# Moving two matrix operands 64 bytes further: g at 128 bytes behind y, the turned adjacency at 384 bytes in its room

## The chip, the cores and the metric

The kernel runs on one core of one Trainium2 chip. Four of the core's engines matter here: TensorE (PE in the profile, with its weight loads as PEld), VectorE (DVE), ScalarE (ACT) and the DMA queues. The metric is the device time of one execution in microseconds; each figure is the median of several runs. Within the kernel, addresses count bytes inside one of the 128 partitions of the on-chip memory SBUF; a tile has the same address in every partition.

## What is computed

Sixty-four graphs of 256 nodes with 512 features each pass two layers. All of it is float32.

```
h   = relu(layernorm(x))                       # x: (64, 256, 512)
q, k, v = h Wq^T, h Wk^T, h Wv^T               # 512 x 512 weights
rel = adj^T * (q k^T)                          # 256 x 256 per graph
rel = rel / norm(rel, over the last axis)
x   = x + rel v
h   = relu(layernorm(x))
x   = x + (adj h) W + bias                     # W: 512 x 512
```

## The kernel before

Two graphs are taken at a time, so there are 32 passes (`pairs`, `i` from 0 to 31). With M = Wq^T Wk formed once, a pass does these stages on TensorE, every product written through `mm` (line 255) as "stationary operand times moving operand":

- `g_stage` (line 405): g = M h, turned. Moving operand: h, 512 columns. 48 products.
- `v_stage` (line 416): v. Moving operand: Wv, 512 columns; stationary: h. 48 products.
- `scores` (line 429): the scores q k^T as g times h. Stationary: 128 columns of g; moving: 256 columns of h. 48 products in a pass, 1536 in all.
- `attend` (line 500): normalised scores times v, 512 columns moving.
- `gather` (line 544): y = adj h of the second layer. Stationary: 128 columns of the rows kept in `late` (four of which live in `v_low`); moving: 256 columns of the turned adjacency `adjt`. 32 products in a pass, 1024 in all.
- `mix` (line 571): y times W. Stationary: y; moving: W, 512 columns. 48 products.

Most float32 operands are held as parts named u, l and s (`split_right_ps`, `split_left_ps`), so that three products on parts make one product of nearly full precision. Each product has its own weight load, and the load of the next product's stationary operand runs while the present product streams its moving operand.

The order of instructions on every engine is fixed when the program is built: `Plan.order` simulates the engines with a cost for each operation (0.231 us for a 512-column product, `HALF` = 0.1185 us for a 256-column one) and sorts the operations by the start times it finds. Costs and dependences are named by hand; addresses don't enter.

What matters for the change is where the operands lie. g and y share one room of 2048 + `BEHIND` elements for each part (tags `gy_u`, `gy_l`, `gy_s`): `as_y` takes the first 2048 elements, `as_g` the 2048 that begin `BEHIND` elements later. With `BEHIND` = 16, g begins 64 bytes behind y. The room of the turned adjacency has 512 + 128 elements, and the adjacency begins at element P - 16 = 112 of it, byte 448.

The pool lays the rooms one behind the other in the order in which they are first asked for, each rounded up to 32 bytes. Between the start of `gy_u` and that of `gy_l` lie 8256 bytes of `gy_u`, 384 bytes of layer-norm statistics (two times 96 + 32 + 32 + 32) and 64 bytes of `norms`: 8704 = 17 times 512. Between `gy_l` and `gy_s` lie 8256 + 384 + 64 (`ones` and `low_max`), again 8704. The unused room `level` of 104 elements (416 bytes) brings the rooms behind it back to the same residue. So all large rooms, m, wv, w, h, hs, rel, v_low, late, gy and adjt, begin at one and the same place modulo 512 bytes; call it 0. In that count, modulo 512:

| product | stationary operand | moving operand | distance (stationary minus moving) |
|---|---|---|---|
| all with 512 columns | 0 | 0 | 0 |
| scores | 64 (g) | 0 (h) | 64 |
| gather | 0 (late, v_low) | 448 (adjacency), that is -64 | 64 |

`ident` (for 60 transposes on TensorE), `wq_last`, `wk_last`, `bias_bc` and `low_any` lie between `gy_s` and `level`, 96 bytes off this grid.

Of the kernel before, what the change touches and what calls it, by code (L numbers as in the profile page):

```python
# [113 lines left out]
def kernel(  # L114
# [12 lines left out]
    P = 128  # L127
    B, N, D = x.shape
    DC = D // P
    NC = N // P  # L130
    NB = 2
# [11 lines left out]
    def room(name, *shape, dtype=F32, tag=None):  # L143
        return pool.tile([P, *shape], dtype, name=name, tag=tag or name)

    def parts_room(name, *shape, tag=None):
        return [room(f"{name}_{k}", *shape, dtype=F32R, tag=f"{tag or name}_{k}") for k in "uls"]
# [16 lines left out]

    BEHIND = 16
    w_p = parts_room("w", DC, D)

    def as_y(tile):  # L170
        return tile[:, : DC * T].rearrange("p (d t) -> p d t", d=DC)

    def as_g(tile):
        return tile[:, BEHIND : BEHIND + DC * T].rearrange("p (d t) -> p d t", d=DC)

    def norm_rooms(j):
        return [(room(f"st{j}{n}", TC, 6), room(f"mv{j}{n}", TC, 2), room(f"rs{j}{n}", TC), room(f"nb{j}{n}", TC))
                for n in range(2)]
    wq_room = room("wq_sb", DC * T + BEHIND, tag="gy_u")
    stats = [norm_rooms(0)]  # L180
    norms = [room(f"rn{n}", NB, NC) for n in range(2)]
    wk_room = room("wk_sb", DC * T + BEHIND, tag="gy_l")
    stats.append(norm_rooms(1))
    ones, low_max = room("ones", 1), room("low_max", 1)
    gy_s = room("gy_s", DC * T + BEHIND, dtype=F32R)
    wq_sb, wk_sb = as_y(wq_room), as_y(wk_room)
    low_any = pool.tile([1, 1], I32, name="low_any")
    bias_bc = room("bias_bc", D)
    ident = room("ident", P)
    wq_last, wk_last = room("wq_last", D), room("wk_last", D)  # L190
    room("level", 104)

    rooms = {}

# [25 lines left out]
    def by_pe(i):  # L220

        return i < 2 or i + 1 == NP
# [58 lines left out]
    def load(plan, i, src=None, name="fresh"):  # L281

        dst = fresh if name == "fresh" else ring[i % 2]
        plan.add("SP", 0.65, lambda: SP.dma_start(out=dst, in_=xs[i]), [], keys(name, TC), lands=5.5)
# [24 lines left out]
    def h_rows(plan, i, src=fresh, name="fresh"):  # L309
        relu, needs = norm(plan, i, 0, src, name)  # L310
        for c in range(TC):
            plan.add("ACT", 0.72, lambda c=c: relu(h_rel[:, c, :] if name == "x0" else h_cols[:, c], c),
                     [(name, c), *needs, *([("h_rel", 0)] if c else [])], [("h_rel", c)] if c else keys("h_rel", TC))

    def h_place(plan, early=8.0):
        place(plan, flat_rel, flat_blocks, keys("h_rel", TC), "blocks", 2.3, early)
# [28 lines left out]
    def finish(plan):  # L345
        while waiting:
            waiting.pop(0)()
# [274 lines left out]
    def before_pairs():  # L622
        A.activation(norms[1][:, 0, 0:1], ones, AF.Sqrt)
        for _ in range(8):
            mm(bank[7][:, :P], warm, warm, True)
        V.tensor_single_scalar(low, adj_low[:, 0].bitcast(I32), 0xFFF, op=ALU.bitwise_and)
        V.tensor_reduce(low_max, low, axis=mybir.AxisListType.X, op=ALU.max)
        m_products(0)
        mm(bank[7][0:1, 0:1], low_max, ones, True)
        V.tensor_copy(low_any, bank[7][0:1, 0:1])  # L630
        for m in range(NC):
            for n in range(NC):
                nc.tensor.transpose(bank[6][:, ts(m * NC + n, P)], adj_sb[:, n, ts(m, P)], ident)
        for e in range(1, DC - 1):
            m_products(e)
        plan = Plan()
        h_rows(plan, 0, ring[0], "x0")
        plan.run()

    with tc.manual_schedule(engines=in_order):  # L640
        before_pairs()
    gy = [*(room(f"gy_{k}", DC * T + BEHIND, dtype=F32R) for k in "ul"), gy_s]
    g_p, y_p = [as_g(part) for part in gy], [as_y(part) for part in gy]
    rel_p = [room(f"rel_{k}", NB, NC, NC, P, dtype=F32R) for k in "ul"]
    adjt = []
# [4 lines left out]
    def first_turn(plan):  # L650

        u, l = h
        for d in range(DC):
            ps, key = next_bank(turned=True)

            def go(ps=ps, d=d):
                for c in range(TC):
                    nc.tensor.transpose(ps[:, ts(c, P)], h_rel[:, c, ts(d, P)], ident)
            plan.add("PE", 0.44, go, keys("h_rel", TC), [key])
            plan.add("ACT", 0.49, lambda ps=ps, d=d: A.activation(  # L660
                u[:, d], ps, AF.Copy, scale=NEAR), [key], [("h_u", d)])
            plan.add("DVE", 0.63, lambda ps=ps, d=d: V.tensor_sub(
                l[:, d], ps, f(u[:, d])), [key, ("h_u", d)], [("h_l", d)])
        for k in range(2):
            kept = [(f"h_{q}", d) for q in "ul" for d in (2 * k, 2 * k + 1)]
            plan.add("DVE", 1.14, lambda k=k: h_third(k), kept, [("h_s", 2 * k), ("h_s", 2 * k + 1)])

    def last_m(plan):
        for i in range(DC):
            plan.add("PE", 0.86, lambda i=i: m_products(DC - 1, (i,)), [], [("bank", i)])  # L670
            split_right_ps(plan, bank[i], ("bank", i), [lambda at, q=q: q[:, at, :] for q in m_p],
                           [[("m_u", i)], [("m_l", i)], [("m_s", i)]], i)
# [16 lines left out]
    def turn_wv(plan):  # L689
        for d in range(DC):  # L690
            ps, key = next_bank(turned=True)

            def go(ps=ps, d=d):
                for e in range(DC):
                    nc.tensor.transpose(ps[:, ts(e, P)], wv_sb[:, e, ts(d, P)], ident)
            plan.add("PE", 0.44, go, placed_all, [key])
            split_right_ps(plan, ps, key, [lambda at, q=q: q[:, at, :] for q in wv_p],
                           [[("wv_u", d)], [("wv_l", d)], [("wv_s", d)]], d)

    def split_w(plan):  # L700
        for d in range(DC):
            split_right_ps(plan, w_sb[:, d], [("x1", d)], [lambda at, q=q: q[:, at, :] for q in w_p],
                           [[("w_u", d)], [("w_l", d)], [("w_s", d)]], d)

    def pairs(exact):
        count["bank"] = 4
        waiting.clear()
        rooms.clear()
        plan = Plan()
        turned_adj = room("adjt_r", NC * N + P, dtype=F32R, tag="adjt") if exact else room("adjt", NC * N + P)  # L710
        adjt[:] = [turned_adj[:, P - 16 : P - 16 + NC * N].rearrange("p (c n) -> p c n", c=NC)]
        plan.add("ACT", 0.49, lambda: A.copy(adjt[0].rearrange("p m n -> p (m n)"), bank[6]), [("bank", 6)], ["adjt"])
        first_turn(plan)
        last_m(plan)
        count["bank"] = 4
        turn_wv(plan)
        h_rows(plan, 1)
        h_place(plan, 25.0)
        load(plan, 2)
        first_g(plan)  # L720
        v_stage(plan, 0, exact, (0, 1))
        scores(plan, 0)
        v_stage(plan, 0, exact, (2, 3))
        turn_scores(plan, 0)
        finish(plan)
        h_turn(plan)
        h_parts(plan)
        split_w(plan)
        plan.add("ACT", 0.58, lambda: A.activation(bias_bc, bias_bc, AF.Copy, scale=1.0 / ONE), [], ["bias"])
        attend(plan, 0, exact)  # L730
        for i in range(1, NP):
            last = i + 1 == NP
            load(plan, i, name=f"x{i % 2}")
            if not last:
                h_rows(plan, i + 1)
                h_place(plan)
            if i + 2 < NP:
                load(plan, i + 2)
            g_stage(plan, i)
            v_stage(plan, i, exact, (0,))  # L740
            v_stage(plan, i, exact, (1,), hold=True)
            scores(plan, i)
            gather(plan, i - 1, exact)
            while held:
                held.pop(0)()
            if by_pe(i):
                turn_scores(plan, i)
            v_stage(plan, i, exact, (2, 3))
            if not last:
                if not by_pe(i):  # L750
                    turn_scores(plan, i)
                waiting.append(lambda: (h_turn(plan), h_parts(plan)))
                mix(plan, i - 1)
            attend(plan, i, exact)
            if last:
                mix(plan, i - 1)
                gather(plan, i, exact)
            store(plan, i - 1)
        mix(plan, NP - 1)
        finish(plan)  # L760
        with tc.manual_schedule(engines=in_order):
            plan.run()
# [33 lines left out]
```

## Time and profile before

| what | value |
|---|---|
| median of 3 runs | 1561.38 us (1560.41 to 1562.69) |
| the profiled execution | 1560.76 us |
| its span, first to last instruction | 1559.0 us |
| mean granted TensorE clock | 0.999 |
| scores: matmul rows with 256 columns | 3 x 512, mean 281 ns |
| gather: matmul rows with 256 columns | 896 of late (mean 277 ns), 128 of v_low (mean 283 ns) |
| matmul rows with 512 columns | mean 389 to 391 ns |

Matmuls overlap, so a row's mean duration of one instruction isn't what a product costs. What it costs is the time from its start to the start of the next one. In a timeline, whose rows merge consecutive equal instructions, that is the difference between the starts of two rows divided by the count of the first.

### The profile page before, as it was taken

The numbers are of one execution on the slowest core, as the hardware profiler recorded it, in microseconds if no ns is written. First come the engines' busy times: TensorE is split into PE (matmuls) and PEld (weight loads), VectorE is DVE, ScalarE is ACT, GpSimd is POOL, SyncE is SP. The second block draws the span as 40 slices with busy tenths as digits, with TensorE's granted clock in tenths as the row PEclk, the third lists the DMA queues.
The fourth block names the chain that finished last, engine by engine and source line by source line (L and its number), as shares of the span: only waits on it lengthen the run. The fifth ranks groups of instructions, "written<-read, shape, count | busy, mean of one in ns | idle before, by whom it ended". The sixth has DMA issues, their size and how long they took to land.

```text
span 1559.0 us, 22543 instructions
## 1 busy us (share of the span) xinstructions
PE 1548.2 (99%) x8046; PEld 1323.5 (85%) x8046; DVE 1355.3 (87%) x2419; ACT 1022.7 (66%) x1941; POOL 24.3 (2%) x39
## 2 busy tenths in 40 slices
PE   9999999999999999999999999999999999999998
PEld 6788888888888888888888888888888888888886
DVE  6997889898889988898988899888989888989786
ACT  5567666666667676666676675766666766666654
POOL 0000000000000000000000000000000000000000
PEclk9999999999999999999999999999999999999999
DMA  5321333223333223333233332233332233322211
GB/s 199 112 83 41 122 111 120 77 71 110 118 113 119 66 78 117 114 117 90 72 96 118 112 122 68 77 114 114 116 106 71 81 121 111 120 71 76 85 55 56
DMA packets 91112, 153.63 MB, mean 99 GB/s; under 512 B 17136, under 2 KB 32240, under 8 KB 90992
## 3 DMA queue, kind: packets, MB, share of 16 engines
q1 hardware_dynamic: 80768, 116.46, 24.7%
q0 software_dynamic: 8432, 32.51, 5.7%
q10 hardware_dynamic: 1792, 3.15, 0.6%
q8 instruction: 65, 1.06, 0.3%
q14 instruction: 55, 0.45, 0.1%
HBM read 70.78 MB, written 33.55 MB: 67 GB/s over the span
## 4 chain that ended last, share of the span: by engine, by line
PE 95%; DVE 3%; DMA 1%; ACT 0%; issue 0%; ACTq 0%; DVEq 0%
PE bank L255 95%; DMA bias_bc<-in_L_gnn_bias_dram 1%; DMA x_ring<-in_x_dram 1%; DVE late_parts L266 0%; DVE late_parts L268 0%; DVE rel_s_parts L470 0%; DVE st L292 0%; DVE rel_l L475 0%; DVE gy_l L275 0%; DVE m_l L268 0%; DVE gy_l L268 0%; DVE wv_l L268 0%; DVE ht L322 0%; DVE wv_s L266 0%; DVE m_s L266 0%
## 5 line engine op out<-in xcount | busy, mean ns | idle before, releaser
L361 ACT ACTIVATE bank<-bank 128x512 f32<-128x512 f32 x572 | 333.5, 583 | 307.8 <-PE bank L255 304.2
L255 PE MATMUL bank<-wv_s,hs 128*128 128x512 f32 x512 | 137.8, 391 | 0.0
L255 PE MATMUL bank<-wv_u,h_u 128*128 128x512 f32 x512 | 137.5, 390 | 0.0
L255 PE MATMUL bank<-wv_l,h_l 128*128 128x512 f32 x512 | 136.9, 389 | 0.0
L255 PE MATMUL bank<-w_u,gy_u 128*128 128x512 f32 x512 | 136.9, 389 | 0.0
L255 PE MATMUL bank<-w_l,gy_l 128*128 128x512 f32 x512 | 136.9, 389 | 0.0
L255 PE MATMUL bank<-h_l,m_l 128*128 128x512 f32 x512 | 136.6, 389 | 0.1
L255 PE MATMUL bank<-w_s,gy_s 128*128 128x512 f32 x512 | 136.7, 389 | 0.0
L255 PE MATMUL bank<-h_u,m_u 128*128 128x512 f32 x512 | 136.5, 389 | 0.0
L255 PE MATMUL bank<-hs,m_s 128*128 128x512 f32 x512 | 136.4, 389 | 0.0
L266 DVE SCALAR_TENSOR_TENSOR gy_s<-gy_u,bank 128x512 fp32r<-128x512 f32 x128 | 86.2, 675 | 43.0 <-ACT gy_u L265 43.0
L255 PEld LDWEIGHTS bank<-h_l,m_l 128*128 128x128 f32 x512 | 96.0, 188 | 20.4 <-DVE h_l L339 0.5
L255 PEld LDWEIGHTS bank<-wv_l,h_l 128*128 128x128 f32 x512 | 96.1, 188 | 20.2
L255 PEld LDWEIGHTS bank<-h_u,m_u 128*128 128x128 f32 x512 | 96.0, 188 | 20.2 <-ACT m_u L265 0.2
L255 PEld LDWEIGHTS bank<-w_l,gy_l 128*128 128x128 f32 x512 | 96.1, 188 | 20.0
L255 PEld LDWEIGHTS bank<-hs,m_s 128*128 128x128 f32 x512 | 96.1, 188 | 19.9
L255 PEld LDWEIGHTS bank<-w_u,gy_u 128*128 128x128 f32 x512 | 96.0, 188 | 20.0
L255 PEld LDWEIGHTS bank<-w_s,gy_s 128*128 128x128 f32 x512 | 96.0, 188 | 20.0 <-ACT bank L361 0.2
L255 PE MATMUL bank<-adjt_r,late_parts 128*128 128x256 f32 x896 | 112.6, 277 | 0.0
L255 PEld LDWEIGHTS bank<-wv_s,hs 128*128 128x128 f32 x512 | 93.8, 188 | 18.3 <-ACT bank L361 0.7
L255 PEld LDWEIGHTS bank<-wv_u,h_u 128*128 128x128 f32 x512 | 93.7, 188 | 17.7
L255 PEld LDWEIGHTS bank<-adjt_r,late_parts 128*128 128x128 f32 x896 | 107.3, 188 | 0.0
(110 smaller groups left out, 3072.3 us busy)
## 6 DMA issues: line engine op xcount, KB each, us to landing
fresh<-in_x_dram SPq DMA_DIRECT2D x31, 1024.0 KB, 5.7
blocks<-h_rel SPq DMA_DIRECT2D x496, 64.0 KB, 2.0
x_ring<-in_x_dram SPq DMA_DIRECT2D x31, 1024.0 KB, 8.0
out_dram<-x_ring POOLq DMA_DIRECT2D x31, 1024.0 KB, 5.4
h_rel<-h_rel SPq DMA_DIRECT2D x464, 32.0 KB, 1.8
blocks<-in_L_gnn_Wv_dram ACTq DMA_DIRECT2D x1, 1024.0 KB, 11.1
x_ring<-in_L_gnn_weight_dram SPq DMA_DIRECT2D x1, 1024.0 KB, 12.3
out_dram<-x_ring SPq DMA_DIRECT2D x4, 256.0 KB, 2.3
```

The lines of the kernel that those rows point to most:

```text
L255: nc.tensor.matmul(out, left, right, start=first, stop=True, skip_group_check=True)
L266: plan.add("DVE", 0.63, lambda: V.scalar_tensor_tensor(s(), f(u()), ONE, ps, op0=ALU.mult, op1=ALU.subtract), [*key, *ku], ks)
L361: plan.add("ACT", 0.49, lambda: A.activation(ps, ps, AF.Copy, scale=ONE), [], [key])
```

## The change

`BEHIND` becomes 32, so g begins 128 bytes behind y, and the rooms of `gy` grow by 64 bytes each. The adjacency begins at element P - 32 = 96 of its room, byte 384. `norms`, `ones` and `low_max` move behind `gy_s`, which leaves 8320 + 384 = 8704 bytes between the starts of the gy rooms, and `level` shrinks by 192 bytes, which is what the three gy rooms have grown. All rooms ahead of `gy_u` and behind `level`, and the three gy rooms themselves, keep their addresses; `bias_bc`, `ident`, `wq_last`, `wk_last` and `low_any` move by 192 bytes. No operation is added, removed or put in another order.

```diff
-    BEHIND = 16
+    BEHIND = 32
...
     stats = [norm_rooms(0)]
-    norms = [room(f"rn{n}", NB, NC) for n in range(2)]
     wk_room = room("wk_sb", DC * T + BEHIND, tag="gy_l")
     stats.append(norm_rooms(1))
-    ones, low_max = room("ones", 1), room("low_max", 1)
     gy_s = room("gy_s", DC * T + BEHIND, dtype=F32R)
     wq_sb, wk_sb = as_y(wq_room), as_y(wk_room)
+    norms = [room(f"rn{n}", NB, NC) for n in range(2)]
+    ones, low_max = room("ones", 1), room("low_max", 1)
...
-    room("level", 104)
+    room("level", 56)
...
-        adjt[:] = [turned_adj[:, P - 16 : P - 16 + NC * N].rearrange("p (c n) -> p c n", c=NC)]
+        adjt[:] = [turned_adj[:, P - 32 : P - 32 + NC * N].rearrange("p (c n) -> p c n", c=NC)]
```

In the count of the table above, after the change:

| product | stationary operand | moving operand | distance |
|---|---|---|---|
| all with 512 columns | 0 | 0 | 0 |
| scores | 128 (g) | 0 (h) | 128 |
| gather | 0 (late, v_low) | 384 (adjacency), that is -128 | 128 |

## The prediction

> **What bounds the kernel now.** First the busy times and the chain of work that ended last:
>
> ```profile
> PE 1548.2 (99%) x8046; PEld 1323.5 (85%) x8046; DVE 1355.3 (87%) x2419; ACT 1022.7 (66%) x1941; POOL 24.3 (2%) x39
> ...
> PE 95%; DVE 3%; DMA 1%; ACT 0%; issue 0%; ACTq 0%; DVEq 0%
> ```
>
> TensorE never rests and is 95% of the chain. The waits of TensorE confirm it: the longest in total is 1.2 us, once, on the DVE. So what counts is the sum of the start-to-start times of 8046 products, and a nanosecond on each 256-column product (1536 in scores, 1024 in gather) is 2.56 us.
>
> Next the timeline of TensorE through the 256-column part of an ordinary pass (start, duration, what, count):
>
> ```profile
> 600.38 1.07 PE L255 MATMUL bank<-wv_l,h_l 128*128 128x512 f32 x4
> 601.28 1.07 PE L255 MATMUL bank<-wv_s,hs 128*128 128x512 f32 x4
> 602.19 1.11 PE L255 MATMUL bank<-h_u,gy_u 128*128 128x256 f32 x8
> ...
> 604.08 1.09 PE L255 MATMUL bank<-wv_s,hs 128*128 128x512 f32 x4
> 605.00 1.10 PE L255 MATMUL bank<-h_u,gy_u 128*128 128x256 f32 x8
> ...
> 607.83 0.40 PE L255 MATMUL bank<-adjt_r,v_low 128*128 128x256 f32 x2
> 608.07 0.85 PE L255 MATMUL bank<-adjt_r,late_parts 128*128 128x256 f32 x6
> 608.76 1.10 PE L255 MATMUL bank<-hs,gy_s 128*128 128x256 f32 x8
> 609.70 0.40 PE L255 MATMUL bank<-adjt_r,v_low 128*128 128x256 f32 x2
> 609.94 2.66 PE L255 MATMUL bank<-adjt_r,late_parts 128*128 128x256 f32 x22
> ```
>
> Read it by differences of starts. The eight 512-column products from 600.38 to 602.19 cost 226 ns each. The 24 scores from 605.00 to 607.83 cost 117.9 ns each. The 22 gathers from 609.94 to 612.43, where the next row begins, cost 113.2 ns each, half of a 512-column product. In between, the gathers just behind scores cost 120 (two in 0.24 us) and 115 (six in 0.69 us). So equal work at an equal distance of 64 bytes has two prices, 113.3 and 117.9 ns. One pass shows the prices the other way round; it is the one behind a disturbed start:
>
> ```profile
> 130.60 1.07 PE L255 MATMUL bank<-h_u,gy_u 128*128 128x256 f32 x8
> 131.50 1.07 PE L255 MATMUL bank<-h_l,gy_l 128*128 128x256 f32 x8
> 132.41 1.07 PE L255 MATMUL bank<-hs,gy_s 128*128 128x256 f32 x8
> 133.32 0.40 PE L255 MATMUL bank<-adjt_r,v_low 128*128 128x256 f32 x2
> ...
> 135.42 2.75 PE L255 MATMUL bank<-adjt_r,late_parts 128*128 128x256 f32 x22
> 138.01 0.39 PE L255 MATMUL bank<-wv_u,h_u 128*128 128x512 f32 x1
> ```
>
> Here, with the same addresses, 24 scores cost 2.72 us (113.3 ns each) and 22 gathers 2.59 us (117.7 each). The price hangs on the address and also on a phase that is carried along from stage to stage. With these addresses the two stages answer it oppositely: whichever is dear, the other is cheap. That is the fact on which I build.
>
> **The parts of the change.** *Operations.* None is added or removed, and since the planner knows no addresses, every queue, those of SP and POOL included, keeps its order and each instruction its waits. Cost 0; nothing need cover it.
>
> *Engines other than TensorE.* DVE writes g 64 bytes off the grid at 692 ns (gy_l from line 268) and late on the grid at 692 ns; it reads the adjacency 64 bytes off at 691 ns (line 444) against 687 ns for a like operation on the grid (line 541). Cost 0, with a bound of 4 ns on any of the 64 score maskings, 0.3 us, which hides under TensorE: at 87% busy the DVE isn't on the chain but for 3%. Without that cover 0.3 us would be the cost.
>
> *Rooms that move by 192 bytes.* `ident` feeds 60 transposes, `wk_last` and `wq_last` 8 products. The widest spread that the trace shows between prices of one product is 4.6 ns (117.9 - 113.3), so 68 times that, 0.3 us either way. I take 0.
>
> *Scores and gather: the price of 2560 products at distance 128.* The trace holds no stage at that distance, so I bound it by the prices of 256-column products above. Now, per pass: scores 48 x 117.9 = 5.66 us, gather 0.24 + 0.69 + 0.24 + 2.49 = 3.66 us.
>
> - Low end, all at 113.3 ns, the cheapest row: scores save 48 x 4.6 = 0.22 us a pass, 7.1 us over 32 passes. Gather falls to 32 x 113.3 = 3.63, 0.03 a pass, 1.0 in all. The four 512-column products inside scores cost 0.92 us (604.08 to 605.00) against 4 x 226.25 = 0.905, 0.5 in all. The twelve behind gather take 2.74 us (612.43 to 615.17) against 12 x 226.25 = 2.715, 0.8 in all. Sum -9.4 us.
> - High end, all at 120 ns, the dearest row (v_low): scores +2.1 x 48 x 32 = +3.2; gather 32 x 120 = 3.84, +0.18 a pass, +5.8; the twelve products behind a dear gather took 2.77 us (138.01 to 140.78) against 2.74, +0.03, +1.0. Sum +10.0 us.
> - The value I take: 117.9 for both stages. What is particular now is that the two stages have shifted operands of different kinds: in scores the stationary operand stands 64 bytes off the grid, in gather the moving one, and a stage follows the other with the opposite price. After the change both operands of both stages stand at multiples of 128. A phase that helps one stage can then no longer be the one that hurts the other. The phase that the 512-column products (226 ns, both operands on multiples of 128) hand to scores today is the dear one in the ordinary passes, and nothing in the trace says that it would be another. Scores: 0. Gather: 32 x 117.9 = 3.77, +0.11 a pass, +3.6 us. Behind gather +0.03 a pass, +1.0. Sum +4.6 us.
>
> On the profiled execution (1560.76, of which 1559.0 is span and 1.8 us lie around it, untouched) that makes 1565.4. It ran 0.6 us under the median of 1561.4, so the forecast is 1566.0 as a median.
>
> A rule against any of this stands in the Trainium skill, page "TensorE: Matmul & The Clock Gate", section on what each phase is for: a weight load and the moving operand have independent read ports, so that the load of the next weights takes nothing from the running product. By it the distance is indifferent and the change gives 0, 1561.4 us. The rows at 113.3 and 117.9 ns for equal products don't fit a rule without interference, though they don't show where the interference lies. The same page gives N/2.4 + 2.5 ns for back-to-back products, an estimate of 109 ns for 256 columns; no row here is below 113, and 109 everywhere would put the sum near 1543.
>
> **The rivals.** *All cheap.* With every operand on a multiple of 128, the 256-column products are like the first half of a 512-column one, which runs at 226 ns without extra. If the phase that these are locked in carries over unharmed, scores and gather both run at 113.3 and the low end holds: 1561.4 - 9.4 = 1552.0. For it: half of 226 is 113, and the swapped pass shows that scores can run at that price. Against it: a 512-column product leaves the weight load twice the time, so a disturbed load needn't show there at all. The deciding point is the mean over all 256-column products: now (1536 x 117.9 + 1024 x 114.4)/2560 = 116.5 ns, and below that the change wins. If only scores turn cheap and gather dear, as in the swapped pass, this is not reached: from 605.00 to 612.43 the ordinary pass needs 7.43 us, and from 130.60 to 138.01 the swapped one 7.41.
>
> *No difference.* Either the distance has no say and the phase alone decides, or the stages swap prices: 0.02 us a pass, 0.6 in all, 1561 us. For it: both prices occur at one address. Against it: the prices repeat in nearly every pass, and to the row, so something fixed sets them.
>
> *Dearer than forecast.* Distance 128 costs more than what the trace holds steadily, up to the 120 ns of the products just behind a switch: 1571.4. It is the upper part of my forecast's side, not a case of its own.
>
> **How the numbers follow.** Slower, at 117.9 or above in both stages: 0.50. All cheap, or so much of it that the mean falls clearly under 116.5: 0.30. No difference: 0.20. The predicted time is the likeliest case, 1566.0, whose own range is 1564.5 to 1571.4. The full range runs from the all-cheap 1552.0 to 1571.0; prices never seen in the trace are left outside. Runs of this kernel spread over 2.3 us, and about 0.2%, 3.1 us, is what can be told from no change; by that line the forecast at +4.6 counts as slower and the swap as the same.
>
> **What would show it.** In the timeline of an ordinary pass of the changed kernel, 24 consecutive scores should take 2.83 us and 22 consecutive gathers 2.59 instead of 2.49; the 512-column rows away from these stages should stay at 0.905 us for four. Scores at 2.72 us with gathers at 2.49 mean the all-cheap rival. Scores at 2.72 with gathers at 2.59 mean a swap. Rows near 2.9 for 24 scores mean the dear end. The prediction is wrong at its root if the 512-column rows change, if TensorE begins to wait, or if the two stages still have opposite prices.

## The result and the profile after

| | before | after |
|---|---|---|
| median of 6 runs each, us | 1561.53 | 1567.78 |
| ratio, 95% interval | | 1.0039 [1.0028, 1.0049] |
| profiled execution / its span, us | 1560.76 / 1559.0 | 1567.37 / 1565.6 |

The change costs 6.25 us, 0.4%. Five of the six runs after lie between 1567.37 and 1567.91; the sixth was a slow one of 4033 us that the ratio leaves out, and the record doesn't say what slowed it.

The busy times and the chain of the changed kernel:

```profile
span 1565.6 us, 22543 instructions
...
PE 1554.8 (99%) x8046; PEld 1330.5 (85%) x8046; DVE 1355.8 (87%) x2419; ACT 1022.4 (65%) x1941; POOL 24.3 (2%) x39
...
PE 95%; DVE 3%; DMA 0%; issue 0%; ACT 0%; DVEq 0%
```

The same instructions, the same chain, and PE busy 6.6 us longer, as much as the span has grown. TensorE's longest wait is still one of 1.2 us. So nothing waits more; products cost more. The timeline of TensorE through an ordinary pass of the changed kernel (start, duration, what, count; a product's cost is the difference of starts):

```profile
603.47 1.08 PE L255 MATMUL bank<-wv_s,hs 128*128 128x512 f32 x4
604.38 1.13 PE L255 MATMUL bank<-h_u,gy_u 128*128 128x256 f32 x8
...
606.30 1.09 PE L255 MATMUL bank<-wv_s,hs 128*128 128x512 f32 x4
607.22 1.13 PE L255 MATMUL bank<-h_u,gy_u 128*128 128x256 f32 x8
...
610.11 0.40 PE L255 MATMUL bank<-adjt_r,v_low 128*128 128x256 f32 x2
610.35 0.88 PE L255 MATMUL bank<-adjt_r,late_parts 128*128 128x256 f32 x6
611.07 1.11 PE L255 MATMUL bank<-hs,gy_s 128*128 128x256 f32 x8
612.02 0.40 PE L255 MATMUL bank<-adjt_r,v_low 128*128 128x256 f32 x2
612.25 2.77 PE L255 MATMUL bank<-adjt_r,late_parts 128*128 128x256 f32 x22
614.86 1.08 PE L255 MATMUL bank<-wv_u,h_u 128*128 128x512 f32 x4
```

The 24 scores from 607.22 to 610.11 now take 2.89 us (120.4 ns each), the 22 gathers from 612.25 to 614.86 take 2.61 (118.6 each). Before it was 2.83 (117.9) and 2.49 (113.2). Both stages have become dear, scores too. And the pass behind the disturbed start, which before had the prices the other way round, now has the ordinary ones:

```profile
130.49 1.13 PE L255 MATMUL bank<-h_u,gy_u 128*128 128x256 f32 x8
131.46 1.12 PE L255 MATMUL bank<-h_l,gy_l 128*128 128x256 f32 x8
132.42 1.13 PE L255 MATMUL bank<-hs,gy_s 128*128 128x256 f32 x8
133.38 0.40 PE L255 MATMUL bank<-adjt_r,v_low 128*128 128x256 f32 x2
...
135.52 2.77 PE L255 MATMUL bank<-adjt_r,late_parts 128*128 128x256 f32 x22
138.12 1.08 PE L255 MATMUL bank<-wv_u,h_u 128*128 128x512 f32 x4
```

24 scores take 2.89 us here too, 22 gathers 2.60. With start-to-start times added up over the whole trace: scores 180.8 us before and 184.2 after, gather 117.6 and 121.6, all other products 1253.3 and 1252.5. That is +3.4, +3.9 and -0.7, together the 6.6 us by which the span grew.

### The profile page after: what moved, and what is told of

Read it like the earlier page. It is cut to its first block, busy times and chain, and to the rows that moved or that the text cites. A ratio compares the mean times of both kernels' runs of the same rounds, so it can differ in the third digit from the quotient of the medians.

```text
span 1565.6 us, 22543 instructions
## 1 busy us (share of the span) xinstructions
PE 1554.8 (99%) x8046; PEld 1330.5 (85%) x8046; DVE 1355.8 (87%) x2419; ACT 1022.4 (65%) x1941; POOL 24.3 (2%) x39
## 4 chain that ended last, share of the span: by engine, by line
PE 95%; DVE 3%; DMA 0%; issue 0%; ACT 0%; DVEq 0%
PE bank L255 95%; DMA fresh<-in_x_dram 0%; DVE late_parts L266 0%; DVE late_parts L268 0%; DVE rel_s_parts L470 0%; DVE st L292 0%; DVE gy_l L275 0%; DVE rel_l L475 0%; DVE m_l L268 0%; DVE wv_l L268 0%; DVE ht L322 0%; DVE wv_s L266 0%; DVE m_s L266 0%; DVE w_l L268 0%; DVE h_l L339 0%
## 5 line engine op out<-in xcount | busy, mean ns | idle before, releaser
L255 PE MATMUL bank<-adjt_r,late_parts 128*128 128x256 f32 x896 | 116.7, 282 | 0.0
L255 PEld LDWEIGHTS bank<-adjt_r,late_parts 128*128 128x128 f32 x896 | 110.9, 188 | 0.0
```

The source lines that it names most:

```text
L255: nc.tensor.matmul(out, left, right, start=first, stop=True, skip_group_check=True)
```

## The experiments

All twelve keep the computation whole. In the tables below, "24 scores" and "22 gathers" are the longest unbroken rows of an ordinary pass, read off the timeline; "scores" and "gather" are the sums over a pass of 48 and 32 products, medians of the 31 passes with both stages in the trace, from the starts in nanoseconds.

### Which part does it

g alone (the adjacency stays at byte 448):

```diff
-        adjt[:] = [turned_adj[:, P - 32 : P - 32 + NC * N]...
+        adjt[:] = [turned_adj[:, P - 16 : P - 16 + NC * N]...
```

(on the changed kernel)

> Only g is moved to 128 bytes behind y; the adjacency stays at byte 448. If each stage pays by its own distance alone, scores cost what they cost after the change (24 in 2.89 us, 120.4 ns each, against 2.83 before), gather stays at 113.2 ns, and the time lies about half way: some 3 us above before, 1564.5. If the two stages are coupled by a phase that the one hands to the other, scores are at 117.9 to 120.4 and gather is not bound to stay cheap: the 22 gathers in a row cost 2.59 us or more, and the time is 1567 or above. If the moved rooms are the cause, 1567.8.

The adjacency alone: the kernel before with `P - 32` for `P - 16`.

> Only the adjacency is moved to byte 384; g stays 64 bytes behind y and no room moves. Own distance alone: scores stay at 117.9 ns (24 in 2.83 us), 22 gathers cost 2.61 us as after the change, time about 3.5 us above before, 1565. Coupled by phase: gather at 118 ns, and scores can change too, to 113.3 (24 in 2.72 us) or 120; the time is then 1558 to 1568. If the moved rooms are the cause, 1561.5.

The rooms of the changed kernel with the operands of the one before: `BEHIND` = 32 and the new order of rooms, but

```diff
-        return tile[:, BEHIND : BEHIND + DC * T]...
+        return tile[:, BEHIND - 16 : BEHIND - 16 + DC * T]...
```

and the adjacency at `P - 16`.

> The rooms lie as after the change (norms, ones, bias_bc, ident and the last weights moved), g and the adjacency as before. If the operands of the 256-column products are the cause: 1561.5 within 1 us, 24 scores in 2.83 and 22 gathers in 2.49 us. If the moved rooms are the cause: 1567.8.

Distance 0: the changed kernel's rooms, g where y begins, the adjacency at element `P`, byte 512.

> g begins where y begins and the adjacency at a multiple of 512, so that the distance of all 256-column products is 0. If what counts is that both operands stand on multiples of 128 bytes, this is like the changed kernel: 24 scores in 2.83 to 2.89 us, 22 gathers in 2.59 to 2.61, time 1566 to 1569. If the price rises with the distance from 64 or falls with it, so that 0, 64 and 128 lie on one line, distance 0 is cheaper than before: 1555 or below. If it depends on how close the operands are, 0 is dearer than 128: 1570 or above.

| kernel | time, us | ratio to before (1562.21) | 24 scores | 22 gathers | scores | gather |
|---|---|---|---|---|---|---|
| before | 1562.21 | | 2.83 | 2.49 | 5.65 | 3.67 |
| changed | | | 2.89 | 2.61 | 5.76 | 3.80 |
| g alone | 1564.41 | 1.0011 [1.0002, 1.0021] | 2.88 | 2.51 | 5.76 | 3.65 |
| adjacency alone | 1565.12 | 1.0017 [1.0007, 1.0026] | 2.82 | 2.62 | 5.63 | 3.80 |
| rooms alone | 1562.31 | 1.0001 [0.9991, 1.0010] | 2.83 | 2.50 | 5.65 | 3.67 |
| distance 0 | 1568.84 | 1.0040 [1.0026, 1.0055] | 2.86 | 2.64 | 5.74 | 3.84 |

The moved rooms do nothing. Each shifted operand makes its own stage dear, by nearly as much as in the whole change. With g alone:

```profile
606.47 1.13 PE L255 MATMUL bank<-h_u,gy_u 128*128 128x256 f32 x8
607.43 1.12 PE L255 MATMUL bank<-h_l,gy_l 128*128 128x256 f32 x8
608.39 1.13 PE L255 MATMUL bank<-hs,gy_s 128*128 128x256 f32 x8
609.35 0.39 PE L255 MATMUL bank<-adjt_r,v_low 128*128 128x256 f32 x2
609.58 0.84 PE L255 MATMUL bank<-adjt_r,late_parts 128*128 128x256 f32 x6
```

24 scores at 2.88 us, 120 ns each, and the gathers right behind them at 0.23 us for two and 0.68 for six, 113 to 115 ns: even the 120 ns that the first gathers cost before are gone. With the adjacency alone:

```profile
610.01 1.08 PE L255 MATMUL bank<-hs,gy_s 128*128 128x256 f32 x8
610.92 0.40 PE L255 MATMUL bank<-adjt_r,v_low 128*128 128x256 f32 x2
611.15 2.78 PE L255 MATMUL bank<-adjt_r,late_parts 128*128 128x256 f32 x22
613.77 1.09 PE L255 MATMUL bank<-wv_u,h_u 128*128 128x512 f32 x4
```

22 gathers take 2.62 us, and the eight scores between two gather blocks 0.91, 114 ns each, where they cost 0.94 before: the cheap price of distance 64 shows up in scores when products at another distance go ahead of them. So the coupling by a phase exists, but it is small: +2.2 and +2.9 us for the parts alone against +6.25 for the whole, of which some 1 us is left for it, within the intervals. The sums over a pass leave as much: scores and gather together +0.24 us in the changed kernel, +0.09 with g alone and +0.11 with the adjacency alone, so 0.04 a pass. On the parts alone, own distance was the better theory; the coupled one, 1567 or above for g alone, missed. Distance 0 came out as dear as 128, which ends the theory of a price on one line through 0, 64 and 128 (1555 or below).

### The place or the distance

A room of 64 bytes is put in front of all others in the kernel before:

```diff
+    room("front", 16)
     fresh = room("fresh", TC, D)
```

> A room of 64 bytes in front of all others moves every operand of before by 64 bytes; the distances stay as before. If only the distance between the operands counts: scores 5.65 and gather 3.67 us a pass as before, time 1561.5 within 1 us. If the operands' own places count (multiples of 128 bytes or not), the stages swap their prices or both change: gather 3.80, scores 5.45 to 5.76 us a pass.

1562.87 us beside 1562.83 for the kernel before, 24 scores in 2.82, 22 gathers in 2.50, sums 5.65 and 3.67: to the nanosecond as before. Modulo 512 gather now has the places that scores had, the stationary operand at 64 and the moving one at 0, and keeps its own price. Moving both operands by 64 bytes is indifferent (no other common shift was run); what counts is how far the two of a product stand from each other.

### The price of a distance

For larger distances the gy rooms get 112 elements more than y instead of 16, with two fillers that keep them level modulo 512; `BEHIND` and the adjacency's first element are then free.

> g 32 bytes behind y, the adjacency at byte 480, distance 32. If the price depends on 64-byte blocks that both operands are in, this is like distance 0: gather 120 ns each (3.84 us a pass), scores 5.74. If it falls with any offset, it lies between distance 0 and 64: gather 3.67 to 3.84, scores 5.65 to 5.74.

> g 192 bytes behind y, the adjacency at byte 320, distance 192. If being off a multiple of 128 bytes is what makes it cheap, this is like before: scores 5.65, gather 3.67 us a pass, 1561.5. If the price rises with the distance from 64 on, it is dearer than the changed kernel: above 5.76 and 3.80, time above 1568.

> g 448 bytes behind y, the adjacency at byte 64: distance -64, the moving operand ahead of the stationary one in the 512-byte count. If the sign has no say, like before: 5.65 and 3.67 us a pass. If the moving operand, which is read in twice the length, runs into the weights from behind at distance 64, it is free of that at -64: scores at 113.3 ns, 5.44, gather 3.63, time 1553 to 1555. If it meets them near the end instead, 120 ns: 5.76 and 3.84, 1569.

> Scores at distance 80 bytes, gather at 96. So far 256-column products cost 120 ns at distance 0, 118.2 at 32, 113.3 or 117.8 at 64, 118.4 to 120.4 at 128, 117.8 at 192 and -64. If 64 is the one low point, scores and gather lie between 113.3 and 120, and nearer to 118: scores 5.55 to 5.76, gather 3.67 to 3.80 us a pass, time 1562 to 1567. If the low point lies beyond 64, both run at 113.3: scores 5.44, gather 3.63, time 1553 to 1555.

> The same two distances with the stages exchanged: scores at 96, gather at 80. If each stage pays for its own distance, scores here cost a product what gather cost at 96 in the run before, and gather what scores cost at 80, within 1 ns. If the stages are coupled by a phase, they differ by more.

> Scores at distance 48, gather at 160. If 64 is the low point: scores between the 118.2 of distance 32 and the 113.3 to 117.8 of 64, 5.45 to 5.68 us a pass; gather 117.8 to 118.4 as at 128 and 192, 3.77 to 3.80. If multiples of 64 bytes are special, both cost 118 to 120.

The times, one run each beside one of before: 1566.90, 1565.58 and 1566.07 (before 1562.83), then 1565.40, 1567.60 and 1566.55 (before 1561.67). Put together, by distance, from the long rows (10 ns of reading are 0.4 ns here):

| distance, bytes | a score, ns | a gather, ns | from |
|---|---|---|---|
| 0 | 119.2 | 120.0 | distance 0 |
| 32 | 118.8 | 118.2 | d32 |
| 48 | 117.5 | | g48_a160 |
| 64 | 117.9 | 113.2 | before |
| 80 | 118.3 | 119.1 | g80_a96, g96_a80 |
| 96 | 118.8 | 117.7 | g96_a80, g80_a96 |
| 128 | 120.4 | 118.6 | after |
| 160 | | 120.0 | g48_a160 |
| 192 | 117.5 | 117.7 | d192 |
| -64 (448) | 117.9 | 118.2 | dm64 |

Of the ten, 64 is the only distance at which 113 ns occurs. All others cost 117.5 to 120.4, whether above or below. They aren't fixed to the nanosecond either: rows of eight scores or more at one distance differ by up to 2.4 ns (at 128, in the changed kernel, 120.4 in the row of 24 and 118.0 in that of 8; at 96, 118.6 in the row of 24, 117.3 in that of 16 and 119.4 in that of 8; medians from the starts). Several expectations missed: 192 is neither like 64 nor dearer than 128; -64 is no better; 160 costs 120, not 118. The kernels at 192 and -64, which are 256 bytes apart, have the same sums a pass (5.65 and 3.77), and a pass of both from the first score to the end of the last gather takes 10.36 us, alike to a nanosecond. That fits a pattern that repeats every 256 bytes, on this one pair alone. The exchanged runs at 80 and 96 agree within 1.1 ns between scores and gather, at 96 just over the 1 ns that was set, so they don't decide between own price and phase. The last rows of distance 192, for comparison with the 2.49 of distance 64:

```profile
612.22 2.75 PE L257 MATMUL bank<-adjt_r,late_parts 128*128 128x256 f32 x22
614.81 1.09 PE L257 MATMUL bank<-wv_u,h_u 128*128 128x512 f32 x4
```

### Handing the cheap phase on

If products at another distance leave behind them the phase in which distance 64 is cheap, then 16 of the scores at 128 could buy cheap prices for the rest:

```diff
-    g_p, y_p = [as_g(part) for part in gy], ...
+    g_p, y_p = [as_g(part, at) for part, at in zip(gy, (32, 16, 16))], ...
-    v_low = room("v_low", 4, D, dtype=F32R)
+    v_low = room("v_low", 4 * D + P, dtype=F32R)[:, 16 : 16 + 4 * D].rearrange("p (r d) -> p r d", r=4)
```

(on the changed kernel, with the adjacency at `P - 16`)

> Only g's upper part (gy_u) stands at distance 128, its other two parts and the adjacency at 64, and the rows of v_low stand 64 bytes further, so that the v_low products of gather are at 128. If distance 64 has two prices and products at 128 just ahead hand over the phase of the cheap one: the gy_u products cost 120.4 ns, the gy_l and first gy_s products behind them 113.3 (8 in 0.91 us instead of 0.94), gather is cheap as with g alone at 128 (3.65 us), a pass gains some 0.08 us, and the time is 1.5 to 3.5 us under before. If every stage pays for its own distance alone: gy_l and gy_s stay at 117.8 ns, gather at 3.67 or above, a pass loses 0.04 us or more, time 1 to 3 us over before.

```profile
604.46 1.12 PE L255 MATMUL bank<-h_u,gy_u 128*128 128x256 f32 x8
605.42 1.07 PE L255 MATMUL bank<-h_l,gy_l 128*128 128x256 f32 x8
606.33 1.09 PE L255 MATMUL bank<-wv_s,hs 128*128 128x512 f32 x4
...
609.12 1.07 PE L255 MATMUL bank<-hs,gy_s 128*128 128x256 f32 x8
610.03 0.40 PE L255 MATMUL bank<-adjt_r,v_low 128*128 128x256 f32 x2
...
612.13 2.76 PE L255 MATMUL bank<-adjt_r,late_parts 128*128 128x256 f32 x22
614.73 1.09 PE L255 MATMUL bank<-wv_u,h_u 128*128 128x512 f32 x4
```

The handing on works: eight gy_u products cost 0.96 us (120 ns), the eight gy_l behind them 0.91 and the eight gy_s 0.91 (114 ns), at the distance at which they cost 118 before. Scores fall to 5.59 us a pass. But the long row of gathers is then dear, 2.60 us for 22, so the passes gain nothing (+0.02 us), and the kernel takes 1566.26 against 1561.79 us, ratio 1.0029 [1.0018, 1.0041]. The other 4 us went to `attend`, where v_low is the moving operand of 512-column products and now stands 64 bytes off its partners:

```profile
630.18 0.63 PE L255 MATMUL bank<-v_low,rel_u 128*128 128x512 f32 x2
630.66 0.39 PE L255 MATMUL bank<-v_low,rel_l 128*128 128x512 f32 x1
...
636.21 1.07 PE L255 MATMUL bank<-h_u,m_u 128*128 128x512 f32 x4
```

From 630.18 to 636.21 the stage takes 6.03 us. In the kernel before, the same products took 5.90, with this first pair:

```profile
627.86 0.61 PE L255 MATMUL bank<-v_low,rel_u 128*128 128x512 f32 x2
628.32 0.39 PE L255 MATMUL bank<-v_low,rel_l 128*128 128x512 f32 x1
...
633.76 0.61 PE L255 MATMUL bank<-h_u,m_u 128*128 128x512 f32 x2
```

0.48 us for the two instead of 0.46, and 0.13 over the stage, 4.2 us in 32 passes. No version here beat the kernel before.

## Why the prediction was right, and where it was not

The direction and the cause held: slower, by dearer 256-column products, in a kernel where TensorE hardly waits. Step by step:

- **Bound and order.** As predicted: the same 22543 instructions, no new wait, the 512-column rows away from these stages unchanged (602.56 to 603.47: 0.91 us for four).
- **Operations, other engines, moved rooms, each 0.** Confirmed: the rooms alone took 1562.31 against 1562.21, and the DVE reads the adjacency at 692 ns instead of 691 and is 3% of the chain in both.
- **Gather +3.6.** Measured +3.9, and 2.61 us for the 22 where 2.59 was to show. The size was near, but partly by luck: the reason given for it fell, as said below.
- **Behind gather +1.0.** Not there. The twelve 512-column products took 2.73 us (614.86 to 617.59) against 2.74 before; all products outside the two stages together got 0.7 us cheaper.
- **Scores 0.** This is the term that was mis-sized. I let them stay at 117.9, the dear price of distance 64, as if that were the dear price of any distance. At 128 it is 120.4: +3.4 us. My high end, 120 ns in both stages, described scores better than the value I took.
- **Sum +4.6, 1566.0.** Measured +6.25, 1567.8, inside the forecast's own range. Two slips in the working don't touch it: the full range ends at 1571.0 where its own sum gives 1571.4, and the widest spread is put at 4.6 ns though the row at 120 makes it 6.7, under 0.5 us for the 68 products concerned.

The fact on which I built was that two stages have opposite prices and swap them. What it foretold came: at distance 128 both are dear, and the pass behind the disturbed start no longer swaps. But the fact itself holds only in part, as another pass of the kernel before shows:

```profile
794.74 1.10 PE L255 MATMUL bank<-h_u,gy_u 128*128 128x256 f32 x8
...
797.56 0.40 PE L255 MATMUL bank<-adjt_r,v_low 128*128 128x256 f32 x2
...
799.72 2.75 PE L255 MATMUL bank<-adjt_r,late_parts 128*128 128x256 f32 x22
802.31 1.09 PE L255 MATMUL bank<-wv_u,h_u 128*128 128x512 f32 x4
```

Here 24 scores take 2.82 us and 22 gathers 2.59: at distance 64 both are dear at once. In the whole trace the long row of gathers is dear three times in 32 (the third time at the very end, with no scores beside it), and the 24 scores are cheap in one pass alone.

The reason I gave fell as well. I argued from the operands' places, one stage having the stationary operand off the grid and the other the moving one. With everything shifted by 64 bytes no price of an ordinary pass changed; places don't enter there. What is particular to before is its distance: 64 is the only one of the ten at which a long row reaches 113 ns, and the change left it.

Of the rivals, *all cheap* failed on both stages, and *no difference* on the fixed prices of 128. The Trainium skill's rule of independent read ports ("TensorE: Matmul & The Clock Gate", section on what each phase is for) doesn't survive as a rule of equal prices: like instructions cost 113.2 to 120.4 ns by the distance and by the products ahead of them.

Two things stay open. The first is which weights interfere. Within a stage, a product's own weights and those loaded during it stand at the same distance from the moving operand modulo 512, so the prices there don't show it. One place in the traces does, at the edge of a stage. Ahead of the first scores of a pass runs a row of four 512-column products of wv_s and hs, whose own operands are at distance 0 in every kernel here; while the last of them streams, the first weights of g are loaded. From its start to the next product's start it takes 226 ns (median of 32 passes) with g at distance 64, 192 or 448, 227 at 0, 228 at 96, 232 to 233 at 48 and 128, and 235 at 32 and 80. The product before it takes 227 ns in all of them. So the place of the next weights has a price of its own, up to 9 ns there, which the product's own operands can't explain. Whether it is the running product that is slowed or the start of the next that is held up isn't shown, nor whether a product's own weights matter too inside a stage. The second is why 64 has two prices, and what the phase is that is carried over; shown is only that products ahead can hand it on.

## What to carry to other kernels

Where TensorE is the bound and products are short, the distance in bytes between stationary and moving operand is a parameter to be measured: here it moved a 256-column product between 113 and 120 ns, and the kernel by 0.4%. Read such prices as differences of starts in unbroken rows of the timeline, where one profile resolves what many runs hardly do, and measure each stage by its own rows. Don't take the dearest price seen at one distance for a ceiling at another, and before moving an operand look for every other product that it takes part in.

## What the runs showed that I had not expected

- Shifting all operands together by 64 bytes changes nothing, to the nanosecond in a pass (10.25 us from the first score to the last gather, in both).
- Distance 64 has two stable prices, 113 and 118 ns, and the products ahead can turn a stage from one to the other. At the other distances long rows kept between 117 and 120.4.
- A 512-column product whose own operands don't move gets up to 9 ns dearer by the place of the weights that are loaded during it.
- A 512-column product is not immune: with v_low 64 bytes off, `attend` lost 0.13 us of 5.90 a pass.
